# Attention's numerators copied by VectorE, and the end of a convolution rearranged

## The chip, the cores and the metric

The kernel runs on one core of a Trainium2 chip. The metric is the device time of one execution in microseconds (us), the median of several runs. A core has five engines that run side by side and wait for each other through semaphores: TensorE (matrix products; PE in the profile, its weight loads PEld), VectorE (DVE), ScalarE (ACT), GpSimd (POOL) and SyncE (SP, which issues transfers). Products land in PSUM[...]; everything else lies in SBUF. All values here are 32-bit floats.

## The reference, cut to what matters

Two layers work on x, four images of 256 channels and 48 x 48 points (N = 2304). The change touches the first one alone:

```python
x = lax.conv_general_dilated(Vx, conv_w, window_strides=(1, 1), padding='SAME', dimension_numbers=('NCHW', 'OIHW', 'NCHW'))
x = x + conv_b[None, :, None, None]
...
x = jax.nn.relu(x)
...
qkv = jnp.einsum('oc,bchw->bohw', qkv_w, x) + qkv_b[None, :, None, None]
qkv = qkv.reshape(B, h, 3 * d, N)
q, k, v = (qkv[:, :, :d], qkv[:, :, d:2 * d], qkv[:, :, 2 * d:])
attn = jax.nn.softmax(jnp.einsum('bhdn,bhdm->bhnm', q, k) * scale, axis=-1)
out = jnp.einsum('bhem,bhnm->bhen', v, attn).reshape(B, C, H, W)
out = jnp.einsum('oc,bchw->bohw', proj_w, out) + proj_b[None, :, None, None]
```

There are 8 heads of 32 channels. The left-out lines are a batch normalization. The second layer convolves with filters that depend on the point ("dynamic filters"); in the kernel its work is interleaved with the next image's convolution.

## The kernel before

**Stages.** For each image b (0 to 3) the kernel computes the 3 x 3 convolution and its ReLU (`hid`), then q, k and v (tiles pq and pv), then a bound on the scores (pb), then attention, then the projection. While the convolution, q, k and v of images 1 to 3 are computed, the dynamic filters of the image before run between them: `far`, `near`, `prod`, `wb` and `py` are theirs. In attention no other stage has products on TensorE but the projection.

**Attention** (`attention`, from line 1305). The queries are cut into 9 units: 8 units of 512 queries for four heads at once, and a unit 8 that holds the last 256 queries of both groups of four heads. A unit has NT = 18 steps, one for each 128 keys. One step m does:

- `scores` on TensorE (line 1340): `so` for the first head and `se` for the other three. `so` has one PSUM buffer, `se` two.
- two exponentials on ScalarE (lines 1350 and 1351) into the tile p. There are four buffers for p; a plan (`home`) gives step 4 of a unit the buffer that step 0 had, step 5 that of step 1. Some steps are "lent" (`LENT = (2, 5, 8, 11, 14)`, in unit 0 only 9 and 14): a transfer that POOL issues (lines 1392 and 1394) adds three heads' part of p to a second accumulator, and VectorE adds only the first head's 512 columns.
- `weigh` of the step before: TensorE adds p times v to `num` (line 1375), which has one PSUM buffer, and VectorE adds p to `acc` (line 1390), from which the denominators come. The first add of a unit, at step 1, reads the p of steps 0 and 1 together.

So the order on TensorE is: scores of step m, weighing of step m - 1, scores of step m + 1. Step 17 of a unit is weighed after step 0's scores of the next unit. After it VectorE adds the lent part (line 1397), and ScalarE copies `num` to `ao` (line 1400). The weighing of the next unit's step 0 writes `num` anew, and so waits for this copy. `close` divides: a unit's denominators are summed by TensorE (`den`, line 1406), then VectorE transposes, takes reciprocals, transposes back and multiplies (lines 1418 to 1428). A unit is closed at step 1 of the unit after the next, unit 7 at step 2 of unit 8.

In unit 8 two products write different columns of one `num` buffer. Before the first of them, products with a tile of zeros start the accumulation over all 512 columns (line 1372, four products an image; two entries each in the profile, as every 32-bit product has):

```python
                if several and m == 0:

                    for j, r in enumerate(heads):
                        nc.tensor.matmul(st["num"][r, :], zeros, p[:, j, :], start=True, stop=False)
```

**The convolution of images 1 to 3** (`conv_blocks`, from line 1108) is a sum of transformed products: six row terms i in the order 1, 2, 3, 4, 0, 5, each for two halves o of the output channels (12 tiles, `TILES`), and four column products n = 0 to 3 for each tile. The first two column products are combined to `two` (their sum and difference), the last two are added to it and give the row term y. For the row terms 0 and 5 y is added to a combination of the others (s12 or d12) and goes through ReLU to `hid`. The last tile, i = 5 and o = 1, is thus the last thing that q and k wait for: `before` computes d12 ahead of it with two operations (line 1074), `after` adds d12 to y, and `relu` follows. `either` gives an element-wise operation to POOL or VectorE by a clock that the program keeps of its own estimates while it is built (`clock`); `busy_dve` by the same clock lets ScalarE move a product out of PSUM (lines 1191, 1196, 1207) where VectorE is behind. The convolution's products, q, k and v share two PSUM buffers.

**The bound.** After the last of v's products (line 1278), one product of `top` with a constant (line 1294) and a VectorE copy (line 1295) leave a bound, which is read only at the end of the kernel.

Of the kernel before, what the change touches and what calls it, by code (L numbers as in the profile page):

```python
# [8 lines left out]
F32 = mybir.dt.float32  # L9
F32R = mybir.dt.float32r  # L10
AF = mybir.ActivationFunctionType
ALU = mybir.AluOpType
# [5 lines left out]
P = 128  # L18
# [40 lines left out]
def conv_preact_kernel(  # L59
# [493 lines left out]
    with tc.tile_pool(name="w", bufs=1) as wpool, tc.tile_pool(  # L553
# [554 lines left out]
        def conv_blocks(b, psum_tile, blocks, pool, hid):  # L1108

            axpy = blocks.axpy  # L1110
            tt = nc.vector.tensor_tensor
            rows = hid.rearrange("p h (t r w) -> p h t r w", r=4, w=WW)
            spare = list(blocks.spare)

            results, last = [], [0.0]

            def busy_dve():
                return clock.t["DVE"] > max(clock.t["ACT"], clock.t["PE"]) + 500

            def relu(o, r, y, end):  # L1120
                results.append((o, r, y, end))

            def relus(limit):
                while results and results[0][3] + 150 <= limit:
                    o, r, y, end = results.pop(0)
                    nc.scalar.activation(  # L1126
                        rows[:, o, :, r, :], rows_of(y), AF.Relu,
                        bias=bn_t[:, o : o + 1], scale=bn_s12[:, o : o + 1],
                    )
                    clock("ACT", 660, end)  # L1130

            def before(i, o):

                s12, d12, s34, d34 = (blocks.held[:, j, o] for j in range(4))
                if i == 0:
                    t = spare.pop(0)
                    axpy(t, s34, -4.0, s12)
                    relu(o, 2, t, clock.both(800))
                    either(s12, s12, s34, ALU.subtract)
                elif i == 5:  # L1140
# [4 lines left out]
                    clock.both(800)  # L1145

            def target(i, o):

                if i in (1, 3):
                    return blocks.first[o]  # L1150
                if i in (2, 4):
                    return blocks.held[:, 1 if i == 2 else 3, o]
                return spare.pop(0)

            def after(i, o, y):

                s12, d12, s34, d34 = (blocks.held[:, j, o] for j in range(4))
                if i in (2, 4):
                    s, d = (s12, d12) if i == 2 else (s34, d34)
                    either(s, y, blocks.first[o], ALU.add)  # L1160
                    either(d, blocks.first[o], y, ALU.subtract)
                elif i in (0, 5):
                    relu(o, i and 3, y, either(y, y, s12 if i == 0 else d12, ALU.add))

            blocks.scaled()
            need[0] = lambda: 150 + max(slot("c", 2), blocks.end[STEPS[0]])
            for t, (i, o) in enumerate(TILES):
                u = us.pop(t)
                y = target(i, o).rearrange("p (n s) -> p n s", s=2)
                for n, j in enumerate((1, 2, 0, 3)):  # L1170
                    m = psum_tile(f"pc_{b}_{i}_{o}_{j}")[:, :XN]
                    clock("PE", 0, slot("c", 2), blocks.end[i, j])
                    z = blocks.of[i].rearrange("p (j h n) -> p j h n", j=4, h=NH)[:, j]
                    relus(max(clock.t["ACT"], clock.t["PE"]))
                    for h in range(NH):
                        nc.tensor.matmul(
                            m, u[:, h, j], z[:, h], start=(h == 0), stop=(h == NH - 1)
                        )
                        clock("PE", MM * XN / CH)
                        if h == 0:  # L1180
                            need[0] = lambda: 0.0
                            if n == 0:
                                if t + 2 < len(TILES):
                                    us[t + 2] = taken(t + 2)
                                if t == 0:
                                    blocks.along(ORDER[1])
                                before(i, o)
                            yield MM * XN / CH
                    if n == 0:
                        one = pool.tile([P, XN], F32, tag="one", name=f"one_{b}_{i}_{o}")  # L1190
                        nc.scalar.copy(one, m)
                        end = clock("ACT", 400, clock.t["PE"])
                    elif n == 1:
                        two = pool.tile([P, 2, XN], F32, tag="two", name=f"two_{b}_{i}_{o}")
                        if busy_dve():
                            nc.scalar.copy(two[:, 1], m)
                            end = clock("ACT", 400, clock.t["PE"])
                            either(two[:, 0], one, two[:, 1], ALU.add, end)
                            either(two[:, 1], one, two[:, 1], ALU.subtract, end)
                        else:  # L1200
                            tt(two[:, 0], m, one, ALU.add)
                            tt(two[:, 1], one, m, ALU.subtract)
                            end = clock("DVE", 900, clock.t["PE"], end)
                    else:
                        to = y[:, :, n - 2]
                        if busy_dve():
                            nc.scalar.mul(to, m, 1.0 if j == 0 else -1.0)
                            end = clock("ACT", 450, clock.t["PE"])
                            either(to, to, two[:, n - 2], ALU.add, end)
                        else:  # L1210
                            if j == 0:
                                tt(to, m, two[:, 0], ALU.add)
                            else:
                                tt(to, two[:, 1], m, ALU.subtract)
                            end = clock("DVE", 480, clock.t["PE"])
                        if n == 3:
                            after(i, o, y.rearrange("p n s -> p (n s)"))
# [15 lines left out]
        def conv_qkv(b, gn, psum_tile, weights, ready, pool, between=()):  # L1233
# [40 lines left out]
            for t in range(0, NT, 2):  # L1274
# [15 lines left out]
                    nc.vector.tensor_tensor(top[:, 0], top[:, 0], top[:, 1], ALU.mult)  # L1290
                    nc.vector.tensor_scalar(top[:, 0], top[:, 0], QS, None, ALU.mult)
                yield 4 * MM * C / CH
            pb = psum_tile(f"pb_{b}")
            nc.tensor.matmul(pb[:, :NH], hmat, top[:, 0], start=True, stop=True)
            nc.vector.tensor_copy(bound[:, b, :], pb[:, :NH])  # L1295

        qkv = {}
        CONV_QKV = MM * (6 * 4 * 6 * TN / CH + NCK * NH * 4 + NT * 2 * C / CH)
# [6 lines left out]
        def attention(b, q, k_, vT, pools, spare, project, scratch, following):  # L1305
# [1 line left out]

            ps_s, ps_a, work0 = pools
            ao = keep("h", f"ao_{b}")
            zeros = work0.tile([P, D], F32, tag="zeros", name=f"zeros_{b}", bufs=1)  # L1310
            nc.gpsimd.memset(zeros, 0.0)

            extra = scratch.rearrange("p (j n) -> p j n", j=3)
            scratch = work0.tile([P, QC], F32, tag="rt", name=f"rt_{b}", bufs=1)
# [41 lines left out]
            def weigh(u, m, p):  # L1356
# [6 lines left out]
                several, end = len(units[u]) > 1, u == last  # L1363
                if end and m >= NT - 2:
                    sums(u, p, m == NT - 2, m == NT - 1)
                    if m == NT - 2:
                        sums(u, st["acc"], False, False)
                        sums(u, extra, False, False, 1)
                if several and m == 0:

                    for j, r in enumerate(heads):
                        nc.tensor.matmul(st["num"][r, :], zeros, p[:, j, :], start=True, stop=False)
                for i, (g, q0, n, at) in enumerate(units[u]):
                    for j, r in enumerate(heads):
                        nc.tensor.matmul(  # L1375
                            st["num"][r, at : at + n],
                            vT[:, m, g * P + j * D : g * P + (j + 1) * D],
                            p[:, j, at : at + n],
                            start=(m == 0 and not several),
                            stop=(m == NT - 1 and i == len(units[u]) - 1),  # L1380
                        )
                if end and m >= NT - 2:
                    return
                if m == 0:
                    st["first"] = p
                else:
# [8 lines left out]
                if m == NT - 1 and not end:  # L1395
                    rest = st["acc"][:, 1:]
                    nc.vector.tensor_tensor(rest, rest, extra, ALU.add)
                if m == NT - 1 and not end:
                    g, q0, n, _ = units[u][0]
                    nc.scalar.copy(ao[:, g, q0 : q0 + n], st["num"])  # L1400

            def sums(u, rhs, start, stop, first=0):
                if start:
# [1257 lines left out]
```

## Time and profile before

| what | value |
|---|---|
| time, median of 3 runs (lowest to highest) | 2687.09 us (2684.61 to 2689.64) |
| the profiled execution's own time | 2689.33 us |
| its span in the profile | 2687.6 us |
| mean granted clock of TensorE | 0.989 |
| TensorE busy | 2590.6 us |
| VectorE, ScalarE, POOL busy | 2075.3, 1808.6, 814.3 us |
| attention, unit to unit, image 1 | 37.47, 37.73, 38.57, 41.35, 38.57, 41.36, 38.57, 43.93 us |

The durations used below come from this one profiled execution. A group's line gives its source line, engine, operation, tiles and shapes, then the count, the busy time in us and the mean of one in ns, then the engine's idle time just before the group and what ended it. A line of a timeline gives the start in us from the span's start, the time in us, and the instruction, with the idle time before it in brackets. In the last table of the trace that is used, each line is a stretch of time with each engine's busy time in it (PE, PEld, DVE, ACT, POOL), then the granted clock as a share of full speed.

### The profile page before, as it was taken

The page shows a single profiled execution, that of the slowest core. Times are in us where ns is not written, and L with a number is a line of the kernel's source. Part 1 is how long each engine was busy: PE and PEld are TensorE (multiplying, and loading weights), DVE is VectorE, ACT ScalarE, POOL GpSimd, SP SyncE. Part 2 cuts the span into 40 slices and gives each one's busy share as a digit, 9 for nine tenths or more (in the row PEclk, how much of TensorE's full clock was granted, in tenths as well). Part 3 has the DMA queues.
Part 4 walks back from the last instruction along what each step waited for, and adds up shares of the span by engine and source line. Part 5 has one row for each costly group of instructions (what it writes and reads, how often), then busy time and mean ns, then how long its engine had stood idle before and what let it go on. Part 6 is the DMA issues. An engine that isn't in the chain of part 4 may idle for free. (4 is left out here: it accounts for less than half of the span.)

```text
span 2687.6 us, 42540 instructions
## 1 busy us (share of the span) xinstructions
PE 2590.6 (96%) x16938; PEld 1095.0 (41%) x16938; DVE 2075.3 (77%) x2033; ACT 1808.6 (67%) x2287; POOL 814.3 (30%) x893
## 2 busy tenths in 40 slices
PE   6999999999999999999999999999989999999996
PEld 5642222555562222355555222245546222235554
DVE  7768998757738898967774988985776889895676
ACT  3479888734439899854345998984444889885344
POOL 5201001476520011057751010107765010100453
PEclk9999999999999999999999999999999999999998
DMA  4815445323252445432324354452324544432456
GB/s 164 229 46 107 100 101 115 86 65 100 72 111 70 102 95 112 104 80 79 98 69 85 95 108 105 95 113 78 83 74 120 133 102 99 103 86 75 122 165 221
DMA packets 138094, 279.96 MB, mean 104 GB/s; under 512 B 58152, under 2 KB 98512, under 8 KB 136864
## 3 DMA queue, kind: packets, MB, share of 16 engines
q0 software_dynamic: 27408, 144.00, 23.3%
q1 hardware_dynamic: 110480, 133.17, 18.7%
q8 instruction: 135, 2.21, 0.3%
q14 instruction: 71, 0.58, 0.1%
HBM read 112.12 MB, written 36.04 MB: 55 GB/s over the span
## 5 line engine op out<-in xcount | busy, mean ns | idle before, releaser
L1390 DVE TENSOR_TENSOR acc<-acc,p 128x2048 f32<-128x2048 f32 (+1 forms) x568 | 1039.3, 1830 | 96.2 <-ACT p L1351 44.5
L1351 ACT ACTIVATE p<-se 128x1536 f32<-128x1536 f32 x648 | 938.1, 1448 | 0.0
L1340 PE MATMUL se<-q,k 32*128 32x512 f32 (+1 forms) x4320 | 737.1, 593 | 0.0
L1340 PE MATMUL so<-q,k 32*128 32x512 f32 (+1 forms) x1440 | 728.3, 593 | 3.2 <-DVE bound L1295 2.0
L1375 PE MATMUL num<-p,vT 128*32 128x512 f32 (+1 forms) x5760 | 699.5, 561 | 1.7 <-ACT ao L1400 1.7
L1350 ACT ACTIVATE p<-so 128x512 f32<-128x512 f32 x648 | 388.4, 599 | 158.9 <-PE se L1340 62.7
L1843 POOL TENSOR_TENSOR near<-near,prod 128x384 f32<-128x384 f32 x352 | 353.0, 1037 | 253.6 <-DVE prod L1837 247.6
L1340 PEld LDWEIGHTS so<-q,k 32*128 32x128 f32 x1440 | 216.6, 183 | 517.8 <-ACT p L1350 477.0
L1394 POOL DMA_DIRECT2D ring<-p x128 | 109.1, 852 | 809.3 <-ACT p L1351 545.2
L1375 PEld LDWEIGHTS num<-p,vT 128*32 128x32 f32 x5760 | 129.1, 108 | 475.0 <-issue 448.4
L1837 DVE TENSOR_TENSOR prod<-wb,pad 128x768 f32<-128x768 f32 x192 | 182.0, 954 | 85.1 <-ACT wb L1824 53.7
L1340 PEld LDWEIGHTS se<-q,k 32*128 32x128 f32 x4320 | 227.2, 183 | 5.1 <-ACT p L1351 4.1
L1824 ACT COPY wb<-ws 128x384 f32<-128x384 f32 x216 | 108.8, 507 | 166.7 <-DVE prod L1837 125.6
L1392 POOL DMA_DIRECT2D ring<-p x36 | 20.1, 558 | 560.6 <-ACT p L1351 272.1
L2001 PE MATMUL py<-far,wsc 128*128 128x384 f32 x512 | 169.9, 487 | 0.0
L1545 PE MATMUL pg<-pad,wcat 128*45 128x384 f32 x864 | 146.7, 490 | 8.5 <-ACT lg L1603 8.5
L1256 PE MATMUL pq<-hid,wqkv 128*128 128x384 f32 x384 | 132.6, 500 | 14.2 <-ACT hid L1126 12.0
L1513 ACT COPY far<-far 128x512 f32<-128x512 f32 x86 | 90.3, 1109 | 80.2 <-PE far L1771 76.5
L2001 PEld LDWEIGHTS py<-far,wsc 128*128 128x128 f32 x512 | 96.2, 190 | 66.0 <-issue 1.8
L1256 PEld LDWEIGHTS pq<-hid,wqkv 128*128 128x128 f32 x384 | 73.0, 194 | 68.3 <-ACT hid L1126 14.3
L1390 DVE TENSOR_TENSOR acc<-p,p 128x2048 f32<-128x2048 f32 x36 | 82.3, 2285 | 21.5 <-ACT p L1351 14.6
L1745 DVE COPY_PREDICATED amat<-along_y,bmat 128x768 f32<-128x768 uint32 x72 | 92.0, 1277 | 2.4
(334 smaller groups left out, 2872.6 us busy)
## 6 DMA issues: line engine op xcount, KB each, us to landing
ring<-p POOLq DMA_DIRECT2D x164, 768.0 KB, 5.7
ws<-w_d SPq DMA_DIRECT2D x216, 192.0 KB
ring<-u_d SPq DMA_DIRECT2D x36, 512.0 KB
pad<-in_x SPq DMA_DIRECT2D x14, 1152.0 KB
xst<-in_x POOLq DMA_DIRECT2D x36, 192.0 KB, 3.6
x_d<-pad SPq DMA_DIRECT2D x36, 192.0 KB
u_d<-pad SPq DMA_DIRECT2D x12, 512.0 KB
y_d<-y SPq DMA_DIRECT2D x13, 384.0 KB
```

The lines of the kernel that those rows point to most:

```text
L1256: nc.tensor.matmul(pq[:, :CH], wqkv[:, i, s, g * P : (g + 1) * P], hid[:, i, cols], start=(i == 0), stop=(i == NH - 1),)
L1340: nc.tensor.matmul(dst[:, at : at + n], k_[r, g, m * P : (m + 1) * P], q[r, g, q0 : q0 + n], start=True, stop=True,)
L1350: nc.scalar.activation(p[:, 0, :], s1, AF.Exp, scale=QS)
L1351: nc.scalar.activation(p[:, 1:, :], s3, AF.Exp, scale=QS)
L1375: nc.tensor.matmul(st["num"][r, at : at + n], vT[:, m, g * P + j * D : g * P + (j + 1) * D], p[:, j, at : at + n], start=(m == 0 and not s ...
L1390: nc.vector.tensor_tensor(st["acc"][:, js], other[:, js], p[:, js], ALU.add)
L1394: nc.gpsimd.dma_start(out=extra, in_=p[:, 1:], accum_op=ALU.add)
L1545: nc.tensor.matmul(pg[64 * s : 64 * s + NG, :CH], wcat[:, ii, k, :], shifted(ii, cc, k // 3 - 1, k % 3 - 1), start=(i == 0 and k == 0), st ...
L1824: nc.scalar.copy(pw[:, :CH], fetched[c, k][0])
L1837: nc.vector.tensor_tensor(prod.rearrange("p h (r w) -> p h r w", w=WW), wb, src, ALU.mult)
L1843: nc.gpsimd.tensor_tensor(cat[:, h], cat[:, h], prod[:, h], ALU.add)
L2001: nc.tensor.matmul(py[c][:, o, :CH], wsc[:, n * NH + i, o * P : (o + 1) * P], rhs, start=(n == 0 and i == 0), stop=(n == order[-1] and i = ...
```

## The change

Three things change.

1. The copy of `num` to `ao` moves from ScalarE to VectorE, and stands ahead of the add of step 17 (in the order of instructions: add of step 16, copy, add of step 17, add of the lent part). The zeros and their products go; the first product of a unit starts the accumulation.
2. In the last tile of a convolution (i = 5, o = 1; "base" is d12), d12 is added to the first column product before the second one comes, so that y needs no final add, and the last two column products are read from PSUM by VectorE whatever the clock says. The second column product is added and subtracted in two more operations. In the program as built, POOL does these two for all three images, and VectorE the two sums with d12.
3. The bound is computed after the fifth of the nine pairs of v's products instead of after the last.

```diff
@@ conv_blocks
-            def after(i, o, y):
+            def after(i, o, y, end):
...
                 elif i in (0, 5):
-                    relu(o, i and 3, y, either(y, y, s12 if i == 0 else d12, ALU.add))
+                    if not TILES.index((i, o)) + 1 == len(TILES):
+                        end = either(y, y, s12 if i == 0 else d12, ALU.add)
+                    relu(o, i and 3, y, end)
...
-                                before(i, o)
+                                base = before(i, o)
...
-                    if n == 0:
+                    if n == 0 and base and t + 1 == len(TILES):
+                        one = pool.tile([P, XN], F32, tag="one", name=f"one_{b}_{i}_{o}")
+                        nc.scalar.copy(one, m)
+                        end = clock("ACT", 400, clock.t["PE"])
+                        two = pool.tile([P, 2, XN], F32, tag="two", name=f"two_{b}_{i}_{o}")
+                        for s in range(2):
+                            tt(two[:, s], one, base[0][:, s::2], ALU.add)
+                        base = clock.both(960, base[1], end)
+                    elif n == 1 and base and t + 1 == len(TILES):
+                        if busy_dve():
+                            one = pool.tile([P, XN], F32, tag="one", name=f"uno_{b}_{i}_{o}")
+                            nc.scalar.copy(one, m)
+                            end = clock("ACT", 400, clock.t["PE"])
+                            either(two[:, 0], two[:, 0], one, ALU.add, end)
+                            either(two[:, 1], two[:, 1], one, ALU.subtract, end)
+                        else:
+                            tt(two[:, 0], m, two[:, 0], ALU.add)
+                            tt(two[:, 1], two[:, 1], m, ALU.subtract)
+                            end = clock("DVE", 900, clock.t["PE"], base)
+                    elif n == 0:
...
-                        if busy_dve():
+                        if busy_dve() and t + 1 < len(TILES):
@@ conv_qkv
-            pb = psum_tile(f"pb_{b}")
-            nc.tensor.matmul(pb[:, :NH], hmat, top[:, 0], start=True, stop=True)
-            nc.vector.tensor_copy(bound[:, b, :], pb[:, :NH])
+                if t == 8:
+                    pb = psum_tile(f"pb_{b}")
+                    nc.tensor.matmul(pb[:, :NH], hmat, top[:, 0], start=True, stop=True)
+                    nc.vector.tensor_copy(bound[:, b, :], pb[:, :NH])
+                    free["c"].append(clock("DVE", 200, clock("PE", 100, slot("c", 2))))
@@ attention
-            zeros = work0.tile([P, D], F32, tag="zeros", name=f"zeros_{b}", bufs=1)
-            nc.gpsimd.memset(zeros, 0.0)
...
-                if several and m == 0:
-
-                    for j, r in enumerate(heads):
-                        nc.tensor.matmul(st["num"][r, :], zeros, p[:, j, :], start=True, stop=False)
...
-                            start=(m == 0 and not several),
+                            start=(m == 0 and i == 0),
...
+                if m == NT - 1:
+                    g, q0, n, _ = units[u][0]
+                    nc.vector.tensor_copy(ao[:, g, q0 : q0 + n], st["num"])
...
-                if m == NT - 1 and not end:
-                    g, q0, n, _ = units[u][0]
-                    nc.scalar.copy(ao[:, g, q0 : q0 + n], st["num"])
```

More of the change, by code (lines that the diff above doesn't have):

```diff
@@ L1138, in before @@
                     relu(o, 2, t, clock.both(800))
[L1139 to L1140 removed]
+                    return s12, either(s12, s12, s34, ALU.subtract)
+                if i == 5:
                     t = spare.pop(0)
@@ L1144, in before @@
                     axpy(d12, d34, -8.0, d12)
-                    clock.both(800)
+                    return d12, clock.both(800)
             def target(i, o):
@@ L1205, in conv_blocks @@
                         to = y[:, :, n - 2]
-                        if busy_dve():
+                        if busy_dve() and t + 1 < len(TILES):
                             nc.scalar.mul(to, m, 1.0 if j == 0 else -1.0)
                             end = clock("ACT", 450, clock.t["PE"])
-                            either(to, to, two[:, n - 2], ALU.add, end)
+                            formed = either(to, to, two[:, n - 2], ALU.add, end)
                         else:
@@ L1214, in conv_blocks @@
                                 tt(to, two[:, 1], m, ALU.subtract)
-                            end = clock("DVE", 480, clock.t["PE"])
-                        if n == 3:
-                            after(i, o, y.rearrange("p n s -> p (n s)"))
+                            end = formed = clock("DVE", 480, clock.t["PE"])
+                        if n == 2:
+                            first = formed
+                        else:
+                            after(i, o, y.rearrange("p n s -> p (n s)"), max(first, formed))
                     free["c"].append(end)
@@ L1362, in weigh @@
                 st = state[u]
-                several, end = len(units[u]) > 1, u == last
+                end = u == last
                 if end and m >= NT - 2:
```

## The prediction

> **What bounds the kernel now.** I read the page first (busy time and slices), then the groups with shapes kept apart, then everything that touches the tile num, then the timeline of one unit boundary, engine by engine, and last the ends of the convolutions.
>
> ```profile
> PE 2590.6 (96%) x16938; PEld 1095.0 (41%) x16938; DVE 2075.3 (77%) x2033; ACT 1808.6 (67%) x2287; POOL 814.3 (30%) x893
> L1351 ACT ACTIVATE p<-se 128x1536 f32<-128x1536 f32 x648 | 938.1, 1448 | 0.0
> L1390 DVE TENSOR_TENSOR acc<-acc,p 128x2048 f32<-128x2048 f32 x404 | 925.8, 2292 | 79.5 <-ACT p L1351 44.5 <-DVE acc L1390 1.8
> L1556 DVE COPY lg<-pg 45x384 f32<-45x384 f32 x16 | 9.0, 561 | 47.6 <-ACT lg L1555 47.4
> ```
>
> TensorE sets the time: it is idle for only 97 us. So a change counts only by what it takes from or adds to TensorE. Attention is 648 steps of a regular 2.066 us (scores 1.07, weighing of the step before 1.00). ScalarE needs 0.60 + 1.45 us a step and follows closely. VectorE needs 2.29 us for a full add, more than a step, and catches up only in the steps whose add is cut to 512 columns.
>
> ```profile
> L1400 ACT COPY ao<-num x32: 592/592/595, 193.6 to 2405.5; 128x512 f32<-128x512 f32 x32
> L1372 PE MATMUL num<-p,zeros x32: 592/592/593, 474.7 to 2407.0; 128*32 128x512 f32 x32
>   ACT ao L1400: 14.3, 32
> ```
>
> The third line is who TensorE and its weight loads waited for before num: the copies, 0.45 us each. A boundary is the same in every unit to 0.01 us; this is the one from unit 4 to 5 of image 1, whose first scores start at 997.77. VectorE, ScalarE, TensorE:
>
> ```profile
> 994.69 7.09 DVE L1390 TENSOR_TENSOR acc<-acc,p 128x2048 f32<-128x2048 f32 x3 [0.73 <-ACT p L1351]
> 1001.81 1.76 DVE L1397 TENSOR_TENSOR acc<-acc,ring 128x1536 f32<-128x1536 f32 x1
> 1003.49 0.71 DVE L1418 STREAM_TRANSPOSE rt<-den 128x512 f32<-128x512 f32 x1
> 1005.27 0.69 DVE L1428 TENSOR_TENSOR ao<-ao,rt 128x512 f32<-128x512 f32 x1
> 1005.88 2.28 DVE L1390 TENSOR_TENSOR acc<-p,p 128x2048 f32<-128x2048 f32 x1
> ...
> 1000.75 0.59 ACT L1400 COPY ao<-num 128x512 f32<-128x512 f32 x1
> 1006.46 0.60 ACT L1350 ACTIVATE p<-so 128x512 f32<-128x512 f32 x1 [0.57 <-PE se L1340]
> 1008.53 0.60 ACT L1350 ACTIVATE p<-so 128x512 f32<-128x512 f32 x1
> ...
> 998.84 1.07 PE L1375 MATMUL num<-p,vT 128*32 128x512 f32 x8
> 1002.77 0.69 PE L1340 MATMUL so<-q,k 32*128 32x512 f32 x1
> 1003.25 0.70 PE L1340 MATMUL se<-q,k 32*128 32x512 f32 x3
> 1005.31 0.69 PE L1340 MATMUL so<-q,k 32*128 32x512 f32 x1
> 1007.37 0.69 PE L1340 MATMUL so<-q,k 32*128 32x512 f32 x1
> ```
>
> Here se starts 0.48 us after so, because ScalarE, behind its copy, frees the scores' buffers late; the step from 1002.77 to 1005.31 takes 2.54 instead of 2.07. So the copy costs TensorE 0.47 us a boundary. The last line of VectorE's part is what decides: the new unit's first add (steps 0 and 1) ends at 1008.16, and the exponential of step 4, at 1008.53, overwrites the buffer of step 0 that this add reads. The margin is 0.37 us.
>
> The ends of the convolutions, images 1 to 3 (TensorE's first product that needs the last hid), and the granted clock (PEclk, after POOL's column) before and after the first of these waits:
>
> ```profile
> 736.81 0.59 PE L1256 MATMUL pq<-hid,wqkv 128*128 128x384 f32 x1 [2.15 <-ACT hid L1126]
> 1389.78 1.00 PE L1256 MATMUL pq<-hid,wqkv 128*128 128x384 f32 x1 [2.95 <-ACT hid L1126]
> 2007.58 1.01 PE L1256 MATMUL pq<-hid,wqkv 128*128 128x384 f32 x1 [6.10 <-ACT hid L1126]
> 734.50:737.80 3.30, 1.15 (x5) 0.45 (x5) 2.34 (x2) 1.91 (x3) 2.22 (x2) 1.00 0.12 28
> 737.90:741.20 3.30, 3.30 (x11) 2.04 (x11) 2.50 (x3) 1.77 (x3) 1.91 (x2) 0.50 0.18 60
> ```
>
> TensorE waits 2.15, 2.95 and 6.10 us, and then runs 3.4 us at half clock, which loses another 1.7 us.
>
> **The Trainium skill.** "VectorE: DVE Perf Modes", "Why PSUM operands drop a tier", says that an fp32 operation with a PSUM operand runs at one element a cycle. The trace agrees: 384 columns from PSUM take 561 ns, on the same line as the SBUF add (692 ns at 512 columns, 2292 at 2048: 1.04 ns a column plus 159). "TensorE: Matmul & The Clock Gate", "Architectural detail", says that VectorE's queue is strictly first in, first out, so an early wait holds up all that follows; the trace shows no case of the new wait. "Part 1: The HAM clock gate" of that page ties half clock to windows of about 3.4 us with TensorE idle; the two windows above agree. "Perfetto Trace Analysis", "Optimization Strategy", reads a gap that repeats as a possible lack of room for the next tile; the copy's 0.47 us is one (num has one buffer), and the margin of 0.37 us says that the exponentials' four buffers are nearly another.
>
> **The copy on VectorE.** Removed: 32 ScalarE copies. Added: 32 VectorE copies of 128x512 from PSUM, no row of which exists; 159 + 512 x 1.04 = 692 ns (bounds: 0.55 and 0.85). By the order of instructions it stands between the add of step 16 and the add of step 17, and it waits for the weighing of step 17. Working for the boundary shown:
>
> - weighing 17 ends at 998.84 + 1.07 = 999.91; from a matmul's end to its reader is 0.04 (scores end 998.89, exponential 998.93). The copy runs 999.95 to 1000.64. The add of step 16 was done at 999.38, so VectorE stands idle 0.57 us.
> - the add of step 17 starts at 1000.67 instead of 999.49: 1.18 later. Behind it stand, without a gap, the add of the lent part, the division (two transposes, reciprocal, product) and the first add: this ends at 1008.16 + 1.18 = 1009.34.
> - without ScalarE's copy, step 3 starts at 1002.77 + 2.07 = 1004.84, step 4 at 1006.90, and its exponential is due 1.16 after (as 1007.37 to 1008.53): 1008.06. The buffer is free at 1009.38.
>
> So the exponential of step 4 comes 1.32 us late, and 0.85 later than before. Its long part (1.45 us) ends as TensorE needs it for weighing 4: before, 1009.02 + 1.45 = 1010.47 against a start at 1010.51. That 0.04 is all the slack, so TensorE is 0.82 us later than before at each such boundary, and nothing lets it recover in a stage it bounds. VectorE does recover: it has three gaps of 0.7 us later in a unit, and it is punctual again at step 16. The lent part's add, 1.18 later too, ends at 1004.75, ahead of the lent buffer's next transfer on POOL's queue, which needs step 2's exponentials (1005.89). Boundaries into units 2 to 7, four images: 24 x 0.82 = +19.7 us.
>
> Into unit 1 there is no division, and VectorE is late: the add of step 16 ends 2.65 to 3.16 us after the unit's first scores, where ScalarE's copy started at 2.98. The next weighing moves by -0.22 to +0.29, about 0 over the four.
>
> Into unit 8 the zero products go too. Steps 1 to 3 took 3.80, 2.94 and 2.29; without zeros and copy 2.93, 2.94 and 2.07, 1.09 less. The exponential of step 4 (12.26 after the unit's start) is then due at 11.17, and the buffer is free at 10.39 + 1.18 + 0.04 = 11.61: 0.44 is given back. With the slack: -0.68 x 4 = -2.7 us. The zeros' memset on POOL (0.12 us) was on no path. Attention: +17.0 us.
>
> **The last conv product.** ScalarE loses two evictions (0.43 us each), VectorE the final add (1.43 us) of images 1 and 2; added are two row sums earlier, and one more sum on POOL in images 1 and 2, beside other work. Image 1: prod ends at 733.65, the two sums from PSUM take 0.45 each with overlap (before, 733.57 to 734.39), hid starts at 734.43 instead of 735.89: 1.46 us earlier. The wait falls to 0.7 us, the idle share of that clock window from two thirds to a quarter, and half clock (1.7 us) should go: -3.2. Image 2: VectorE's pair lasted 1.62 beside POOL; now hid starts at 1386.6 instead of 1388.86: -2.3 and again -1.7, -4.0. Image 3 ran its chain on POOL. Now VectorE's row sums can start only after its product at 2004.49 (0.45 each, by VectorE's other sums of 288 columns), then POOL's two sums (1.05 each, between the 0.84 and 1.14 of its rows of that size, to about 2007.2), VectorE's last (0.45), and hid starts at 2007.7 instead of 2006.66: +1.0, of which 0.5 falls into time that was at half clock: +0.5. Together -6.7 (bounds -10 and 0).
>
> **The bound.** The pair of small products (0.42 us) moves among v's products. At the start of attention in images 1 and 2 they lay beside ScalarE's last copy of vT, for which the scores wait anyway; in image 3 TensorE waited 1.99 us until 2082.60, and the statistics of py on VectorE end at 2082.45, so the wait stays but for 0.1. Cost +0.5 (bounds -2 and +1.5).
>
> **Sum.** +17.0 - 6.7 + 0.5 = +10.8 us on the profiled execution, whose span is 2687.6 and whose time is 2689.33, 2.2 above the median of 2687.09. I add it to the median: 2697.9.
>
> **Rivals.** (1) Faster: the release of step 0's buffer isn't the limit, the copy is just gone from ScalarE. Then -0.47 x 24 - 1.09 x 4 - 6.2 = -21.9: 2665. For it: ScalarE's 14.3 us of waits are real. Against: a margin of 0.37 us, and even a copy of no length moves the add of step 17 by 0.49, past it once step 4 comes 0.47 earlier. It decides if the first add still ends by 1008.0. (2) TensorE's pause of some 1.3 us trips half clock in attention: 1.7 us a time; if at a third of 24 boundaries, +14: 2711. For: a window with 2.21 of 3.3 us busy (560.4) was followed by half clock; against: one with 1.78 busy (2502.6) wasn't. (3) The convolution's end brings nothing, as another wait takes the place: 2704.6.
>
> **How the numbers follow.** Likeliest, 0.65: 2698, own range 2692 to 2706 (0.15 us on 24 copies is 3.6, the convolution 4); it holds the third rival. Half clock in attention 0.10, 2706 to 2730. Faster 0.15, 2660 to 2681. In between, gains at the convolutions against small losses, 0.10, 2682 to 2693. About 0.2%, 5.4 us, is what a measurement tells from no change; so faster 0.16, same 0.10, slower 0.74. The range 2682 to 2712 leaves out the first rival and half of the second.
>
> **What would show it.** VectorE's copy of 0.69 us starting 2.2 us after a unit's first scores; the first add ending 11.6 after; ScalarE's exponential of step 4 released by VectorE (line of acc), not by TensorE; TensorE's idle time before the scores of step 5, over 1 us, 24 times or more; waits for hid of about 0.7, 0.7 and 7 us. I am wrong if that exponential still starts 1.16 us after its scores.

## The result, and the profile after

| what | before | after |
|---|---|---|
| median of 4 runs (lowest to highest) | 2687.2 us (2684.61 to 2689.64) | 2707.15 us (2706.57 to 2709.83) |
| the profiled execution: time, span | 2689.33, 2687.6 us | 2707.29, 2705.5 us |
| unit to unit in attention, image 1, units 2, 3 and 7 | 38.57, 41.35, 43.93 us | 39.38, 42.15, 44.74 us |

The changed kernel is slower: the ratio is 1.007, with a 95% interval from 1.0057 to 1.0082. The forecast was 2698, with a range of 2682 to 2712; its likeliest case alone had 2692 to 2706.

First the page's line of busy times, and then, of everything that touches the tile num, the copy's own line and what the engines waited for before these instructions (us, times):

```profile
PE 2595.0 (96%) x16906; PEld 1097.8 (41%) x16906; DVE 2095.4 (77%) x2069; ACT 1792.2 (66%) x2249; POOL 806.9 (30%) x888
L1405 DVE COPY ao<-num x32: 683/692/693, 192.5 to 2422.3; 128x512 f32<-128x512 f32 x32
  PE num L1394: 16.3, 28
  DVE ao L1405: 4.8, 7
```

ScalarE has lost 16 us of work and VectorE has gained 20. TensorE's own busy time is nearly what it was: 2590.6 before, 2595.0 now. So of the 17.9 us by which the span grew, 13.5 are idle time of TensorE. The third line is new: VectorE now waits for the weighing before 28 of its 32 copies, 0.58 us each. The last line is TensorE's wait for the copies, which has fallen from 14.3 us to 4.8. The wait that the change aimed at did go; what is left of it lies at the four boundaries into unit 1.

This is the boundary from unit 4 to unit 5 of image 1, the same one as before. The first scores of unit 5 start at 1005.39. VectorE's lines of the timeline come first, then ScalarE's, then TensorE's:

```profile
1007.60 0.69 DVE L1405 COPY ao<-num 128x512 f32<-128x512 f32 x1 [0.59 <-PE num L1394]
1008.21 2.28 DVE L1412 TENSOR_TENSOR acc<-acc,p 128x2048 f32<-128x2048 f32 x1
1010.52 1.76 DVE L1419 TENSOR_TENSOR acc<-acc,ring 128x1536 f32<-128x1536 f32 x1
1012.20 0.71 DVE L1437 STREAM_TRANSPOSE rt<-den 128x512 f32<-128x512 f32 x1
...
1014.59 2.28 DVE L1412 TENSOR_TENSOR acc<-p,p 128x2048 f32<-128x2048 f32 x1
...
1016.97 0.60 ACT L1373 ACTIVATE p<-so 128x512 f32<-128x512 f32 x1 [1.19 <-DVE acc L1412]
...
1012.67 0.69 PE L1363 MATMUL so<-q,k 32*128 32x512 f32 x1
1012.96 0.70 PE L1363 MATMUL se<-q,k 32*128 32x512 f32 x3
...
1015.02 0.69 PE L1363 MATMUL so<-q,k 32*128 32x512 f32 x1
...
1017.62 0.69 PE L1363 MATMUL so<-q,k 32*128 32x512 f32 x1 [0.46 <-ACT p L1373]
```

Read it from the top. The copy waits, and the adds, the division and the new unit's first add all stand behind it. That first add ends at 1014.59 + 2.28 = 1016.87, 11.48 us after the unit began. Before, it ended after 10.39. ScalarE's exponential of step 4 starts 0.10 after it and names it as what it waited for, at all 24 boundaries into units 2 to 7; before, TensorE's scores released it at all 24. TensorE waits for this exponential in turn before the scores of step 5. A second delay stands in the two lines of 1012.67 and 1012.96: `se` starts 0.29 after `so`. The denominators `den` take one of the two PSUM buffers of `se`, and VectorE's transposition, which reads them, ends only at 1012.91. Steps 1 to 5 take 2.94, 2.28, 2.35, 2.59 and 2.33 us, where they took 2.93, 2.53, 2.07, 2.07 and 2.07. No run takes one of the two waits away alone. That the exponential's, which ends last, sets the total is read from the trace.

In unit 8 two units are closed one after the other. Here `den` decides alone. In image 1 the unit starts at 1131.66 (VectorE's lines, then TensorE's):

```profile
1138.47 0.71 DVE L1437 STREAM_TRANSPOSE rt<-den 128x512 f32<-128x512 f32 x1
...
1143.06 0.71 DVE L1437 STREAM_TRANSPOSE rt<-den 128x512 f32<-128x512 f32 x1
...
1139.24 1.07 PE L1425 MATMUL den<-acc,ones 128*32 128x512 f32 x8 [0.21 <-DVE rt L1437]
...
1143.83 0.49 PE L1363 MATMUL se<-q,k 32*128 32x256 f32 x3 [0.82 <-DVE rt L1437]
```

The second `den` waits for the transposition of the first, and the scores of step 4 wait for the transposition of the second. Steps 1 to 4 take 12.16 us together, where they took 11.10.

The ends of the convolutions of images 1, 2 and 3 on TensorE:

```profile
743.16 0.91 PE L1279 MATMUL pq<-hid,wqkv 128*128 128x384 f32 x2 [0.35 <-ACT hid L1126]
...
1395.50 0.91 PE L1279 MATMUL pq<-hid,wqkv 128*128 128x384 f32 x2 [0.35 <-ACT hid L1126]
...
2018.00 6.23 PE L1279 MATMUL pq<-hid,wqkv 128*128 128x384 f32 x9 [5.43 <-DVE cv_q L1233]
```

Around the first of these waits, two neighbouring stretches (us of busy time on PE, PEld, DVE, ACT and POOL, then the granted clock):

```profile
739.70:743.10 3.40, 2.85 (x14) 1.35 (x12) 2.96 (x5) 1.58 (x4) 1.48 (x2) 1.00 0.29 56
743.15:746.50 3.35, 3.34 (x14) 2.01 (x15) 2.02 (x4) 2.90 (x4) 1.29 (x2) 1.00 0.13 44
```

The waits of 2.15 and 2.95 us have shrunk to 0.35 (with 0.26 more before the product ahead of each), and the stretches of half clock that followed them are gone: the clock stays at 1.00. From the last convolution product to the first scores image 1 takes 69.2 us instead of 71.7, image 2 69.2 instead of 72.4, and image 3 83.5 instead of 83.3.

Put together, the profiled execution changed by:

- attention of the four images, from the first scores to the last weighing: 370.3, 370.8, 370.7 and 372.9 us instead of 365.0, 364.9, 364.9 and 367.3, so +22.6
- convolution's end to the first scores, images 1 to 3: -5.7
- from an attention's end to the last convolution product of images 1 to 3: +2.4. Stretches of half clock, 3.4 us each, fall in other places there than before (with the change at 532, 570, 628 and 1894 us, before at 526, 564, 1178, 1216, 1301 and 1830)
- before the first attention -0.8, after the last -0.7

Before rounding the sum is +17.9, the growth of the span.

### The profile page after: what moved, and what is told of

Its sections match the earlier page's. It is cut to its first block, busy times and chain, and to the rows that moved or that the text cites. A ratio compares the mean times of both kernels' runs of the same rounds, so it can differ in the third digit from the quotient of the medians.

```text
span 2705.5 us, 42465 instructions
## 1 busy us (share of the span) xinstructions
PE 2595.0 (96%) x16906; PEld 1097.8 (41%) x16906; DVE 2095.4 (77%) x2069; ACT 1792.2 (66%) x2249; POOL 806.9 (30%) x888
## 5 line engine op out<-in xcount | busy, mean ns | idle before, releaser
L1856 DVE TENSOR_TENSOR prod<-wb,pad 128x768 f32<-128x768 f32 x192 | 182.0, 954 | 83.5 <-ACT wb L1843 46.7
L1532 ACT COPY far<-far 128x512 f32<-128x512 f32 x86 | 90.4, 1110 | 78.5 <-PE far L1790 76.4
```

Of the source, the lines that this page charges most:

```text
L1856: nc.vector.tensor_tensor(prod.rearrange("p h (r w) -> p h r w", w=WW), wb, src, ALU.mult)
```

## The experiments

The theory: the copy itself is cheap, but its place is not. It waits for the weighing ahead of VectorE's adds, and whatever comes late there releases the buffer of step 0 and the buffer of `den` late. The rivals: VectorE simply has 0.69 us more to do; or the zero products, the bound or the convolution's last tile bring the loss, or hide gains. The first four kernels ran on one chip and the last four on another, each with runs of the kernel before on the same chip: medians of 2691.19 and 2689.6 us. So ratios are compared. A ratio is worked out over all the runs and can differ by 0.1% from the quotient of the two medians.

**The copy back on ScalarE** (against the changed kernel; it keeps its convolution and bound, and has no zero products):

```diff
-                if m == NT - 1:
-                    g, q0, n, _ = units[u][0]
-                    nc.vector.tensor_copy(ao[:, g, q0 : q0 + n], st["num"])
...
                     nc.vector.tensor_tensor(rest, rest, extra, ALU.add)
+                if m == NT - 1 and not end:
+                    g, q0, n, _ = units[u][0]
+                    nc.scalar.copy(ao[:, g, q0 : q0 + n], st["num"])
```

> The changed kernel with the copy of num back on ScalarE, in its old place behind the adds; zeros gone, convolution and bound as changed. Theory (the place of the copy in VectorE's queue delays the unit's first add, and with it the buffer of step 0): units 2 to 7 are as long as before (38.57 and 41.35 us), the wait of ScalarE for acc at step 4 is gone, and attention gives back the 22.6 us that it had lost, and some 2 more where the zeros went: about 2682 us, 2678 to 2687. Rival (the loss comes from the convolution's rearrangement or the bound, and the copy on VectorE is harmless): within 5 us of the changed kernel's 2707.

Measured: 2683.63 us, ratio 0.9981 (0.9966 to 0.9996). The units are 38.57, 41.35 and 43.93 us long again. VectorE's first add, then the exponentials of steps 3 and 4, in unit 5 of image 1, which starts at 991.6:

```profile
999.74 2.28 DVE L1409 TENSOR_TENSOR acc<-p,p 128x2048 f32<-128x2048 f32 x1
...
1000.33 0.60 ACT L1373 ACTIVATE p<-so 128x512 f32<-128x512 f32 x1 [0.58 <-PE se L1363]
1000.82 1.45 ACT L1374 ACTIVATE p<-se 128x1536 f32<-128x1536 f32 x1
1002.39 0.60 ACT L1373 ACTIVATE p<-so 128x512 f32<-128x512 f32 x1
```

The add ends at 1002.02 and the exponential of step 4 starts at 1002.39, with no wait shown: the margin of 0.37 us of the kernel before is back. So the whole loss is the copy's. Unit 8 tells something too. Without zero products its steps 1 to 4 take 2.94, 3.39, 2.08 and 2.65 us: the 0.86 that left step 1 came back in steps 2 and 4, and the sum is 11.06 against 11.10 before. Removing the zero products brought next to nothing even here.

**Only the copy** (against the kernel before: zero products, convolution and bound stay as they were):

```diff
+                if m == NT - 1:
+                    g, q0, n, _ = units[u][0]
+                    nc.vector.tensor_copy(ao[:, g, q0 : q0 + n], st["num"])
                 if m == 0:
                     st["first"] = p
...
-                if m == NT - 1 and not end:
-                    g, q0, n, _ = units[u][0]
-                    nc.scalar.copy(ao[:, g, q0 : q0 + n], st["num"])
```

> The kernel before with nothing changed but the copy, on VectorE and ahead of the add of step 17. Theory: units 2 to 7 last 39.38 and 42.15 us as in the changed kernel, and the time is 22 us above before, 2709 us, 2705 to 2714. Rival (it is the convolution or the bound): within 5 us of 2687.

Measured: 2712.04 us, ratio 1.0081 (1.0064 to 1.0098). The units are 39.38, 42.15 and 44.73 us, as in the changed kernel. Steps 1 to 4 of unit 8 take 3.80, 2.94, 2.29 and 3.13 us: 12.16, the same sum as without zero products. So the copy alone makes the loss.

**The copy behind the add of step 17** (against the changed kernel):

```diff
-                if m == NT - 1:
-                    g, q0, n, _ = units[u][0]
-                    nc.vector.tensor_copy(ao[:, g, q0 : q0 + n], st["num"])
...
                         nc.gpsimd.dma_start(out=extra, in_=p[:, 1:], accum_op=ALU.add)
+                if m == NT - 1 and not end:
+                    g, q0, n, _ = units[u][0]
+                    nc.vector.tensor_copy(ao[:, g, q0 : q0 + n], st["num"])
                 if m == NT - 1 and not end:
                     rest = st["acc"][:, 1:]
```

> The changed kernel with VectorE's copy one place later, behind the add of step 17. VectorE then has no 0.6 us of waiting, since step 17 is weighed long before; but num is free only about 4.75 us after the unit's first scores, 0.7 later than TensorE asks for it. Theory: the first add ends at about 11.1 instead of 11.5, step 4's exponential is late by only some 0.2 behind its own scores, and a boundary costs 0.3 to 0.5 us over before instead of 0.81: units of 38.9 to 39.1 us, about 2695 us, 2690 to 2700. Rival (0.69 us more work on VectorE costs the same wherever it stands): units of 39.4 us, 2707.

Measured: 2702.03 us, ratio 1.0047 (1.003 to 1.0064). Units 2, 3 and 7 fall to 38.76, 41.54 and 44.12 us, so the same copy on the same engine costs 0.19 us there instead of 0.81. That speaks against the rival of VectorE's added work. The wait is another one: TensorE now waits for `num` itself in step 1, which takes 3.59 us instead of 2.94, while steps 2 to 5 are back at 2.07. The median lies above what was expected. What the trace shows for it is the boundary into unit 1, 12.0 us over the four images. VectorE is late there in any case, as no step of unit 0 before step 9 is lent. TensorE's weighing in image 1, and then two neighbouring stretches (us of busy time on PE, PEld, DVE, ACT and POOL, then the granted clock):

```profile
844.59 1.94 PE L1394 MATMUL num<-p,vT 128*32 128x512 f32 x8 [2.64 <-DVE ao L1416]
841.00:844.30 3.30, 0.94 (x8) 0.11 (x5) 3.20 (x3) 2.77 (x3) 0.00 (x0) 1.00 0.01 2
844.40:847.70 3.30, 3.11 (x16) 0.72 (x16) 3.30 (x3) 0.00 (x0) 0.00 (x0) 0.51 0.00 0
```

TensorE waits 2.64 us for the copy here, and 2.60 to 2.65 in the other images. In images 1 and 3 a stretch of 3.4 us at half clock follows (at 844.5 and 2127.9), and unit 1 takes 41.5 us; in images 0 and 2 none follows, and unit 1 takes 39.9, instead of 37.7. Place decides here as well, only at a boundary that had been left out. The profiled execution took 2693.69 us, the shortest of five that reach up to 2710.50; what made the others longer is not shown.

**The add of the lent part later** (against the changed kernel; the copy stays where the change put it, and the add of 1536 columns goes behind the next unit's first add, at the boundaries up to unit 7):

```diff
-                if m == NT - 1 and not end:
+                if m == NT - 1 and u == last - 1:
                     rest = st["acc"][:, 1:]
                     nc.vector.tensor_tensor(rest, rest, extra, ALU.add)
+                if m == 1 and 0 < u < last:
+                    rest = state[u - 1]["acc"][:, 1:]
+                    nc.vector.tensor_tensor(rest, rest, extra, ALU.add)
```

> The changed kernel with the add of the lent part (1.76 us on VectorE) moved behind the next unit's first add, for units 0 to 6; unit 7's stays. The copy stays on VectorE ahead of the add of step 17. Theory: the first add ends 1.8 us earlier, 9.7 after the unit's first scores, ahead of the 10.3 at which step 4's exponential is due; that wait goes and the boundary costs nothing, so at most 24 x 1.28 = 31 us come back: 2676; but the later adds stand as late as in the changed kernel, and the exponentials of steps 6 and 7, whose buffers these free, may wait some 0.3 us each: 2676 to 2688. Rival (TensorE waits for the copy itself or for VectorE's load as a whole): units stay at 39.4 us, 2707.

Measured: 2681.06 us, ratio 0.9967 (0.995 to 0.9985). VectorE's first add and the lent part, then the exponentials of steps 3 and 4, in unit 5 of image 1, which starts at 1001.7:

```profile
1009.08 2.28 DVE L1412 TENSOR_TENSOR acc<-p,p 128x2048 f32<-128x2048 f32 x1
1011.28 1.75 DVE L1422 TENSOR_TENSOR acc<-acc,ring 128x1536 f32<-128x1536 f32 x1
...
1010.11 0.60 ACT L1373 ACTIVATE p<-so 128x512 f32<-128x512 f32 x1 [0.34 <-PE se L1363]
1010.61 1.44 ACT L1374 ACTIVATE p<-se 128x1536 f32<-128x1536 f32 x1
1012.18 0.60 ACT L1373 ACTIVATE p<-so 128x512 f32<-128x512 f32 x1
```

The first add now ends at 1011.36, before the exponential of step 4 is due, and that one waits for nobody. Steps 3 to 5 are back at 2.07 us, and units 2, 3 and 7 take 38.44, 41.09 and 43.67 us, less than before the change. VectorE has as much to do as in the changed kernel. So it is the order of its queue, not its load, that costs. Against the first experiment, with its copy on ScalarE, the units are shorter (38.44 for 38.57, 41.09 for 41.35, 43.67 for 43.93), but the intervals of the two ratios overlap, so the total does not show that the move to VectorE gains anything. Unit 8, whose order is untouched, still takes 12.16 us for steps 1 to 4.

**The copy twice** (against the changed kernel):

```diff
                     nc.vector.tensor_copy(ao[:, g, q0 : q0 + n], st["num"])
+                    nc.vector.tensor_copy(ao[:, g, q0 : q0 + n], st["num"])
```

> The changed kernel with VectorE's copy of num done twice in a row, both ahead of the add of step 17 (1.31 instead of 0.65 us from start to start of what follows). Theory (what stands ahead of the first add is paid in full): units 2 to 7 grow by another 0.6 to 0.7 us, to 40.0 to 40.1 and 42.8; over 24 boundaries and the last units 16 to 20 us above the changed kernel: 2723 to 2727. Rival (TensorE waits for num, or VectorE is only busy longer, which its pauses later in a unit take up): 2707 to 2712.

Measured: 2727.62 us, ratio 1.0147 (1.0129 to 1.0165). The units are 40.11, 42.88 and 45.46 us (+0.73), unit 1 takes 38.37 (+0.8), and steps 1 to 4 of unit 8 take 12.88 (+0.72). The second copy starts 0.73 after the first, so VectorE's time is paid in full and no slack is left anywhere. The exponential of step 4 names its releaser as before:

```profile
1020.78 0.60 ACT L1373 ACTIVATE p<-so 128x512 f32<-128x512 f32 x1 [1.36 <-DVE acc L1413]
```

**The old convolution as well** (the copy back on ScalarE as in the first experiment, and `conv_blocks` of the kernel before; what stays of the change is the missing zero products and the bound amid v's products):

```diff
-                    if n == 0 and base and t + 1 == len(TILES):
...
+                    if n == 0:
...
-                            after(i, o, y.rearrange("p n s -> p (n s)"), max(first, formed))
+                            after(i, o, y.rearrange("p n s -> p (n s)"))
```

> The kernel with the copy back on ScalarE, and the convolution's last tile as before too; zeros gone, bound early. Theory (the rearranged tile is worth 3 us at the end of the convolutions of images 1 and 2, and nothing in image 3; zeros and bound are worth nothing): the stretch from the last product of the convolution to the first scores is again 72 us in images 1 and 2, the time some 5 us above the kernel with the rearranged tile and equal to the kernel before, 2684 to 2690. Rival (the 5 us of that kernel over before come from the zeros' products or the bound): 2680 to 2684.

Measured: 2692.15 us, ratio 1.0004 (0.9995 to 1.0014). From the last convolution product to the first scores images 1 to 3 take 73.1, 73.1 and 83.8 us, where the first experiment took 69.1, 69.1 and 83.4. The half clock after the convolutions of images 1 and 2 is back as well. So zero products and bound together are worth nothing that the total can show, and the convolution's tile is worth about 0.2%, the step from 1.0004 to 0.9981 (two chips, and intervals that only just meet); the traces put it at 3.9, 3.9 and 0.4 us. The three stretches are also 1.3, 0.6 and 0.6 us longer than in the kernel before. In those three stretches the bound is what differs, but one execution of each kernel does not tell how much of it is the bound's.

**Unit 7 divided later** (against the changed kernel; it tests the reading of unit 8 by taking the second `den` out of steps 1 to 3, and the last projection moves with it):

```diff
-                if m == 2 and u == last:
+                if m == 4 and u == last:
...
-                if m == 6 and (u % NH == 1 or u == last):
+                if m == (8 if u == last else 6) and (u % NH == 1 or u == last):
```

> The changed kernel, but unit 7 is divided at step 4 of unit 8 instead of step 2, and the last projection stands at step 8 instead of 6. Theory (in unit 8 the two sums of denominators hold one of the two PSUM buffers of the scores until VectorE, late, transposes them): steps 1 to 4 of unit 8, 12.16 us in the changed kernel, shrink by 1.0 to 1.7 us, 4 to 7 us over four images: 2700 to 2703. Rival (unit 8 is held by the exponentials' buffers as the other units are): steps 1 to 4 stay within 0.3 us, 2706 to 2708.

Measured: 2704.03 us, ratio 1.0054 (1.0037 to 1.0071). Steps 1 to 4 of unit 8 fall from 12.16 to 10.51 us (2.94, 2.28, 2.34, 2.94): where the second `den` is away, its wait is away. But steps 5, 7 and 8 grow to 3.05, 2.30 and 5.11, while step 6 falls from 4.92 to 2.08 as the projection leaves it, so steps 0 to 8 take 25.12 us instead of 25.38. Only 0.26 us an image stays, and the ratio's interval overlaps that of the changed kernel. The cause is confirmed for steps 1 to 4, and the repair is worth almost nothing.

**Both together** (against the changed kernel: the add of the lent part behind the first add at every boundary, unit 7 divided at step 4 and the last projection at step 8):

```diff
-                if m == NT - 1 and not end:
-                    rest = st["acc"][:, 1:]
+                if m == 1 and u:
+                    rest = state[u - 1]["acc"][:, 1:]
                     nc.vector.tensor_tensor(rest, rest, extra, ALU.add)
...
-                if m == 2 and u == last:
+                if m == 4 and u == last:
...
-                if m == 6 and (u % NH == 1 or u == last):
+                if m == (8 if u == last else 6) and (u % NH == 1 or u == last):
```

> The changed kernel with the lent part added behind the next unit's first add at every boundary, unit 7 divided at step 4 of unit 8, and the last projection at step 8. Theory: units 2 to 7 at 38.4, 41.1 and 43.7 us as with the lent part moved alone, and unit 8 shorter by 1 to 2 us an image: 4 to 8 us below that kernel, 2670 to 2676. Rival (another wait in unit 8, the division then being late for the projection): within 3 us of it.

Measured: 2679.79 us, ratio 0.9952 (0.9939 to 0.9965), faster than both kernels. Attention of image 1 takes 364.4 us, against 370.8 with the change and 364.9 before, and steps 0 to 8 of unit 8 take 24.80. The median lies above the 2670 to 2676 expected. Its interval overlaps that of the add moved alone (0.9967), so the part of unit 8 is not shown to add to it.

One thing was not tried: a fifth buffer for p, which would take the wait for step 0's buffer away by itself.

## Why the prediction was right, and where it was not

**The copy and its wait.** Forecast 0.69 us, with 0.57 of idle time ahead of it. Measured 0.692 and 0.59. Right. But rows of such a copy do exist in the kernel before: on line 1515 four copies of 128x512 out of PSUM, `xT` from `xa`, take 691 to 693 ns, and forty of the same size, `far` from `far`, take 1085 in the median. The formula gave the time of the first kind; that the new copy would be of that kind was assumed.

**The boundaries into units 2 to 7.** Forecast +0.82 us each: the first add ends 11.6 us after the unit's start, the exponential of step 4 is late, and TensorE has no slack. Measured +0.81 each, +19.4 us in all; the add ends after 11.48, and the exponential is released by it. Undoing the copy, doubling it and moving what stands behind it all moved this number as the theory has it. The sum was right, but one detail was not. The forecast put the delay into one pause of over 1 us before the scores of step 5. The trace shows 0.46 there, because steps 2 and 3 lose time already: `den` holds a buffer of `se` until VectorE's late transposition. The forecast left that buffer out.

**Half clock in attention** (the second rival). It needed a long pause. The pause came in pieces of 0.46 us and less, and no half clock shows at any of the 24 boundaries. The third experiment, with waits of 2.60 to 2.65 us, tripped it in two of four images.

**Into unit 1.** Forecast about 0. Unit 1 fell by about 0.2 us an image. What is left of attention's +22.6 is 22.6 - 19.4 - 4.2 = -1.0 us over four images: -0.9 from unit 1, +0.2 from unit 0 and -0.3 from the later steps of unit 8.

**Unit 8: the step that failed.** It says: "Steps 1 to 3 took 3.80, 2.94 and 2.29; without zeros and copy 2.93, 2.94 and 2.07, 1.09 less", and then that 0.44 of it "is given back", so -0.68 an image. Measured +1.06 an image: +4.2 us instead of -2.7, the largest error of the sum. The forecast took the release of step 0's p buffer, at 11.61, as the limit. That limit was well placed: the first add ends at 11.48. But a later one stands behind it, the transposition of the second `den`. In the kernel before (unit 8 of image 1 starts at 1121.63) VectorE's line of it and the scores of step 4 read:

```profile
1131.93 0.71 DVE L1418 STREAM_TRANSPOSE rt<-den 128x512 f32<-128x512 f32 x1
...
1132.73 0.49 PE L1340 MATMUL se<-q,k 32*128 32x256 f32 x3
```

The transposition ends at 1132.64, 11.01 us after the unit's start, and the scores that need its buffer start 0.09 later, with no wait shown. In the first experiment (unit 8 from 1115.48) it ends 11.01 after the start as well, at 1126.49. TensorE, without the zero products, is there earlier and has to wait for it: the scores of step 4 start at 1126.55. So the zero products ran in time that would have been a wait. Taking them away gave next to nothing (11.06 against 11.10 us), and VectorE's delay of 1.1 us went straight to TensorE. The lines of before held this. The page "Perfetto Trace Analysis" of the Trainium skill, "Optimizing Tensor Performance", says that matmul groups that don't depend on each other should rotate through different PSUM banks, so that reading one out overlaps the next. Here `den` and `se` take turns in no more than two buffers, and the trace shows a late reader of one stopping the other, by 0.82 us in the wait above.

**The last convolution product.** Forecast -3.2, -4.0 and +0.5 us, with waits for hid of 0.7, 0.7 and 7. The intervals up to the scores, which hold the bound as well, moved by -2.6, -3.3 and +0.2, and the waits were 0.35, 0.35 and 5.43, the last of them ended by VectorE's reading of a product (`cv_q`) and not by hid. With the bound at +0.5 the forecast has -6.2 and the runs -5.7. The mechanism was right in images 1 and 2, half clock included: it goes where the wait goes, and comes back with the old tile. In image 3 the number came close by luck. The forecast had a longer wait; it grew shorter (5.43, after 0.82 and 6.10 before). But the 6.8 us of half clock there fell later: 5.9 us of TensorE's work lie in them (2017.1 to 2023.9), where 3.4 us did (2004.3 to 2011.0). "TensorE: Matmul & The Clock Gate" of the Trainium skill, "Part 1: The HAM clock gate", lets half clock follow a window of about 3.4 us in which TensorE is idle. The trace agrees on the length (3.4 us a stretch) and on the order. On the idleness it agrees less than the forecast says: in the 3.3 us ahead of half clock TensorE was busy for 1.15. The third rival, that this end brings nothing, is refuted.

**The bound.** +0.5 was forecast. Zero products and bound together gave a ratio of 1.0004 (0.9995 to 1.0014), which neither shows such a cost nor rules it out.

**The sum.** +10.8 was forecast for the profiled execution, and the runs show +17.9. Of the 7.1 between, steps 1 to 4 of unit 8 are 6.9, the rest of attention is -1.0, the boundaries are -0.3 (19.4 against 19.7), the convolution's end with the bound is 0.5, and 1.0 lies in the other stretches. The medians differ by 2 us more, as the profiled execution lay 2.1 us above the median before and 0.1 above it after. The measured 2707.15 lies inside the range stated, but 1.2 us outside that of the likeliest case. The stated range reached on to 2712 for half clock in attention, which did not come. So that the total fell into it despite unit 8 is partly luck; the term of the 24 boundaries, which decides the sign, is not. The first rival, that the release of step 0's buffer is no limit, was wrong at all 24.

## What to carry to other kernels

Moving work to an engine whose load has room is not enough: read first how many us early that engine releases what the bound engine needs (here 0.37 and 0.09), and look at every buffer that it releases, PSUM of small side results included. Where the order is free, an instruction that waits is better placed in a queue behind those on which others wait, unless others wait for it too, as in the third experiment. Moving one independent add of 1.76 us out of the way turned +0.7% into -0.3%, where both kernels hold the gain of about 0.2% from the convolution's tile. Before counting products as saved, ask what the next wait would have been without them.

## What the runs showed that was not expected

- A VectorE copy of 128x512 fp32 from PSUM took 692 ns (683 to 693), the same as its add of two SBUF operands of that size, which took 692. Forty other copies of that size, of `far`, took 1085 (1051 to 1110) in the kernel before; why is not shown.
- ScalarE's exponential started 0.10 us after the end of the VectorE add that released its buffer (1016.87 to 1016.97), where it starts 0.04 after the end of scores (998.89 to 998.93 before the change).
- TensorE waits of 2.60 to 2.65 us inside attention (third experiment) were followed by 3.4 us at half clock in two images of four, while a boundary with pauses of 0.46 us and less kept 1.00.
